# Four 64x64 mixing products in place of two column halves, with three PSUM banks shared by two convolution layers

## The chip, the cores and the metric

The kernel runs on one core of one Trainium2 chip. The metric is the device time of one execution in microseconds (us); shorter is better. The kernel before takes 2804.1 us (median of three runs, 2804.09 to 2806.65).

## What is computed

The input is `x` of shape (16, 64, 128, 128) in float32: 16 images of 64 channels. Four residual layers follow one another, each of the form `x = x + layer(group_norm(x))` with 32 groups of two channels:

```python
# layer 0: channel gram matrix, applied to the image, then a 1x1 convolution
gram = einsum('bcn,bdn->bcd', xf, xf) / N
out  = einsum('oc,bchw->bohw', conv_w, einsum('bcd,bdn->bcn', gram, xf))
# layer 1: Scharr filters in x and y on each channel
out  = abs(conv(x, kx)) + abs(conv(x, ky))
# layer 2: a quarter of the channels shifted left, a quarter right, then 3x3 conv, 64 -> 64, + bias
# layer 3: 3x3 conv 64 -> 64, 1x1 conv 64 -> 64, batch norm over the batch, leaky ReLU, clip to 0..255
```

Layer 3 needs statistics over all 16 images before any output can be written, so the kernel has a last part that reads layer 3's result and its input back from HBM, normalizes, adds and stores.

## The kernel before

**Order of the work.** The order is written out by hand. The program is a list of steps, each with four quarters `q` = 0 to 3, and every engine executes its instructions in program order (`InOrder`). An image goes through four stages that run at the same time on different images: `Gram` (layer 0's statistics), `Front` (layers 0 and 1), `Layer2` and `Layer3`. An image is cut into NS = 8 chunks of R = 8 rows for each image half, and in the middle of the run one step handles one chunk of each of Front, Layer2 and Layer3. Within a quarter the order is Layer3, Layer2, Front, then Gram, then `tick()`, which advances the small chains that turn sums into normalization coefficients. On average a step lasts 17.1 us.

**Layer 0 as one product.** Gram leaves for each image a 64x64 matrix that already contains the residual's identity. `abd` holds it twice on the diagonal of a 128x128 matrix, and the two off-diagonal blocks are zero. Front multiplies the input by it; this is called mixing here. A chunk of input is a tile `x` of 128 partitions (64 channels of the upper image half, 64 of the lower) by 8 rows. `mix(i, g)` takes four of the eight rows (512 columns) with `small_product`: one matmul for each column half of the array, 128 rows by 64 columns each. `po` is one PSUM bank. `mix(i + 2, 0)` stands in quarter 1 and `mix(i + 2, 1)` in quarter 3; ScalarE (ACT) reads `po` with `prepare(i + 2, 0)` in quarter 2 and `prepare(i + 1, 1)` in quarter 0 of the next step, and writes `xh`, on which VectorE (DVE) computes layer 1 (`sobel`).

**Layers 2 and 3.** Each is computed from `one`, a product of odd rows that two output rows share, and `two`, a pair of PSUM banks with what each of the two output rows has for itself. `shared` makes `one` with six matmuls, three on each column half. `own(two[:, n], n, ...)` makes one bank of `two` with five matmuls: two on one column half and three on the other, and the next `own` has it the other way round. The order on the matrix engine (PE) in a step is:

- quarter 0: Layer3 `shared`, Layer3 `own` into `two[:, 0]`
- quarter 1: Layer3 `own` into `two[:, 1]`, Front `mix(i + 2, 0)`
- quarter 2: Layer2 `shared`, Layer2 `own` into `two[:, 1]`
- quarter 3: Layer2 `own` into `two[:, 0]`, Front `mix(i + 2, 1)`

ACT copies `one` with a bias to `c`. DVE empties both banks of `two` with a single instruction that adds `c`: `x<-two,c` in quarter 0 for the chunk of Layer2 that ended in the step before (after two small additions, `two<-two,edges`), and `y<-two,c` in quarter 2 for Layer3. Quarter 0 of DVE also has the first two instructions of `sobel`, quarter 1 has four more, and quarters 2 and 3 have one each.

**PSUM.** There are eight banks: `two` has 2 buffers of two banks, and since the layers take turns each has a pair of its own; `one`, `po`, the gram sums `g` and the small products `bank` have one each.

**Other queues.** SyncE (SP) issues the loads and stores. `load` brings a chunk of `x` with two DMAs, one for each image half. GpSimd (POOL) computes edge terms of layer 2 and issues its `qd` copies.

A float32 matmul shows in the trace as two MATMUL records and two weight loads, since it is done in two passes. The trace gives line 73 (the helper of `InOrder`) for nearly every instruction, so groups are told apart by their tiles.

Of the kernel before, what the change touches and what calls it, by code (L numbers as in the profile page):

```python
# [10 lines left out]
F32 = mybir.dt.float32  # L11
# [5 lines left out]
P = 128  # L17
# [91 lines left out]
def tile_kernel(ctx: ExitStack, tc: tile.TileContext, x, cw_h, w2_t, b2, wbin_t, w1_t, b1, gamma, beta, consts, out):  # L109
# [32 lines left out]
    def flat(ap):  # L142
        return ap.rearrange("p j w -> p (j w)")
# [16 lines left out]
    work = ctx.enter_context(tc.tile_pool(name="work", bufs=2))  # L160
    ring = ctx.enter_context(tc.tile_pool(name="ring", bufs=2))
    stp = ctx.enter_context(tc.tile_pool(name="stp", bufs=2))
    ps_two = ctx.enter_context(tc.tile_pool(name="ps_two", bufs=2, space=PSUM))
    ps_one = ctx.enter_context(tc.tile_pool(name="ps_one", bufs=1, space=PSUM))
    ps_po = ctx.enter_context(tc.tile_pool(name="ps_po", bufs=1, space=PSUM))
    ps_g = ctx.enter_context(tc.tile_pool(name="ps_g", bufs=1, space=PSUM))
# [10 lines left out]
    def small_product(dst, wt, src):  # L177

        for o in (1 - last[0], last[0]):
            pe.matmul(dst[cols(o)], wt[:, cols(o)], src, start=True, stop=True)  # L180
        last[0] = o


    bank = ps_sm.tile([P, 512], F32, name="bank")
# [265 lines left out]
    class Front:  # L450
# [11 lines left out]

        def load(self, i):
            b = self.b
            t = xin.tile([P, R, W], F32, tag="x", name=f"x_{b}_{i}")
            for h in range(2):
                sp.dma_start(flat(t[h * C:(h + 1) * C]), halves(x[b].rearrange("c h w -> (c h w)"), h, i * R, R))
            self.xs[i] = t

        def mix(self, i, g):  # L470
            po = ps_po.tile([P, CP, W], F32, tag="po", name=f"po_{self.b}_{i}_{g}")
            small_product(po, self.abd, self.xs[i][:, g * CP:(g + 1) * CP, :])
            self.po[i, g] = po

        def prepare(self, i, g):
            po = self.po[i, g]
            self.normalized(self.chunk(i)[:, 1 + g * CP:1 + (g + 1) * CP, 1:1 + W], po)
            if g == 0 and i > 0:
                self.normalized(self.chunk(i - 1)[:, R + 1, 1:1 + W], po[:, 0, :])
            if g == 1 and i + 1 < NS:  # L480
                self.normalized(self.chunk(i + 1)[:, 0, 1:1 + W], po[:, CP - 1, :])

        def at(self, i, q):
            b = self.b
            if q == 0:
                if i == -3:

                    self.xe = xin.tile([P, W], F32, tag="xe", name=f"xe_{b}", bufs=1)
                    sp.dma_start(self.xe[lo], x[b][:, HH, :])
                    sp.dma_start(self.xe[hi], x[b][:, HH - 1, :])  # L490
                    sp.dma_start(x2_d[b][0:W].rearrange("(p w) -> p w", p=1), w0[0:1, 0:W])
                if i + 3 < NS:
                    self.load(i + 3)
                if -1 <= i < NS - 1:
                    self.prepare(i + 1, 1)
                if 1 <= i:
                    self.store(i - 1)
                    act.activation(
                        junk.rearrange("p (j w) -> p j w", w=W), self.x2.pop(i - 1), AF.Square,
                        accum_out=self.st[:, 1, i - 1:i],  # L500
                    )
                if i == NS:
                    chains.append(coefficients(self.st, lambda co: coefs2.update({b: co}), b2_sb))
            if q == 1 and -2 <= i < NS - 2:
                if i == -2:
                    self.abd, self.co = lead.pop(b)
                    self.pe = ps_g.tile([P, CP, W], F32, tag="g", name=f"pe_{b}")[:, 0, :]
                    small_product(self.pe, self.abd, self.xe)
                self.mix(i + 2, 0)
            if q == 2:  # L510
                if i == -2:
                    nc.gpsimd.memset(self.chunk(0)[lo, 0, :], 0.0)
                    self.normalized(self.chunk(0)[hi, 0, 1:1 + W], self.pe[hi], hi)
                    self.pel = small.tile([P, W], F32, tag="pel", name=f"pel_{b}", bufs=1)
                    self.normalized(self.pel[lo], self.pe[lo], lo)
                if i == NS - 2:
                    nc.gpsimd.memset(self.chunk(NS - 1)[hi, R + 1, :], 0.0)
                    act.copy(self.chunk(NS - 1)[lo, R + 1, 1:1 + W], self.pel[lo])
            if 0 <= i < NS:
                self.sobel(i, q)  # L520
            if q == 2 and -2 <= i < NS - 2:
                self.prepare(i + 2, 0)
            if q == 3 and -2 <= i < NS - 2:
                self.mix(i + 2, 1)
                self.xs.pop(i + 2)

        def sobel(self, i, q):
            b = self.b
# [96 lines left out]
    class Layer2:  # L625
# [57 lines left out]
        def at(self, i, q):  # L683
# [52 lines left out]
            if q == 2:  # L736
                if 0 <= i < NS:
                    t = self.v[i]
                    one = ps_one.tile([P, CP, W], F32, tag="one", name=f"one2_{b}_{i}")
                    two = ps_two.tile([P, 2, CP, W], F32, tag="two", name=f"two2_{b}_{i}")  # L740
                    self.p[i] = two, one
                    shared(one, self.wi[:, 0], t, m)
                    if closing:
                        small_product(one[:, m, :], w0, t[:, R, :])

                    both = self.wi[:, 1]
                    own(two[:, 1], 1, TO_SLOTS, w2, "d2", m, both)
                    if closing:

                        p = two[:, 1, m:CP]  # L750
                        issue([taps(0, p, [both], [t[:, R:R + 1, :]]), taps(1, p, [both], [t[:, R - 1:R, :]])])
                if 1 <= i < NS:
                    self.square(i - 1)
                if 1 <= i:
                    self.store(i - 1)
# [17 lines left out]
    class Layer3:  # L773
# [37 lines left out]
        def at(self, i, q):  # L811
            b = self.b
            n = b * NS + i
            if q == 0 and 0 <= i < NS:
                self.twin(1)
                t = self.v[i]
                one = ps_one.tile([P, CP, W], F32, tag="one", name=f"one3_{b}_{i}")
                two = ps_two.tile([P, 2, CP, W], F32, tag="two", name=f"two3_{b}_{i}")
                self.p[i] = two, one
                shared(one, w3[:, 2], t)  # L820
                own(two[:, 0], 0, TO_PAIRS, w3, "d3")
            if q == 1:
                if 0 <= i < NS:
                    two, one = self.p[i]
                    own(two[:, 1], 1, TO_PAIRS, w3, "d3")
                    self.v.pop(i)
                    self.c = ring.tile([P, CP * W], F32, tag="c3", name=f"c3_{b}_{i}", bufs=1)
                    act.activation(self.c, flat(one), AF.Identity, bias=b1_sb)
                if i + 1 < NS:
                    self.prepare(i + 1)  # L830
                if 1 <= i:
                    y = self.y.pop(i - 1)
                    for s in range(2):
                        for z in range(2):
                            v = pairs(y_d[b], s)[:, (i - 1) * R:i * R, :].rearrange("c (n z) w -> c z n w", z=2)
                            sp.dma_start(v[:, z], y[s * C:(s + 1) * C, z])
            if q == 2:
                if 0 <= i < NS:
                    y = ring.tile([P, 2, CP, W], F32, tag="y", name=f"y_{b}_{i}")
                    self.y[i] = y  # L840
                    two = self.p.pop(i)[0].rearrange("p s j w -> p s (j w)")
                    dve.scalar_tensor_tensor(
                        y.rearrange("p s j w -> p s (j w)"), two, 1.0,
                        self.c.unsqueeze(1).to_broadcast([P, 2, CP * W]),
                        op0=ALU.mult, op1=ALU.add, accum_out=bn_sum[:, n:n + 1],
                    )
                if i + 1 < NS:
                    difference("d3", 0, self.v[i + 1])
            if q == 3:
                if i + 1 < NS:  # L850
                    self.twin(0)
                    difference("d3", 1, self.v[i + 1])
                if 0 <= i < NS:
                    act.activation(
                        junk, self.y[i].rearrange("p s j w -> p (s j w)"), AF.Square,
                        accum_out=bn_sq[:, n:n + 1],
                    )
# [53 lines left out]
    for step in range(steps):  # L911
        for q in range(4):
# [20 lines left out]
            if step == last_one - NS and q == 0:  # L933
                slices(xw.rearrange("p w c t -> p (w c t)"), 8)
                slices(xh.rearrange("p a j w -> p (a j w)"), 3)
                rest(xin, "x", [R, W], 2)
                rest(xin, "xr", [C // 8, W], 3)
                rest(work, "u", [R + 1, W + 2], 2)
                rest(work, "e", [R, W + 2], 1)
# [93 lines left out]
```

## Time and profile before

| | |
|---|---|
| median of three runs | 2804.1 us |
| the profiled execution: its own time | 2800.37 us |
| the profiled execution: span, first to last instruction | 2798.6 us |
| span in which PE is at 9 tenths or more | about 350 to 2330 us |
| last part, DMA at 400 to 420 GB/s, PE idle | about 2350 to 2800 us |
| mixing (`po<-x,abd`) | 1024 records = 512 matmuls, 386.2 us of PE busy time |
| first and last mixing record | 47.3 us and 2102.7 us |
| Gram products (`pg<-xw`) end | about 1740 us |

"Busy" is the time in which at least one instruction of the engine is under way, and a group's busy time is that of its own records. A matmul record's length includes the passage through the array: records of 512 columns last 590 ns, but two that follow one another on the same part of the array start 427 ns apart. The second distance is what a record costs. Two records on different column halves run side by side. A "wait" is idle time of an engine in front of an instruction, put down to what the profile saw arrive last.

### The profile page before, as it was taken

The page shows a single profiled execution, that of the slowest core. Times are in us where ns is not written, and L with a number is a line of the kernel's source. Part 1 is how long each engine was busy: PE and PEld are TensorE (multiplying, and loading weights), DVE is VectorE, ACT ScalarE, POOL GpSimd, SP SyncE. Part 2 cuts the span into 40 slices and gives each one's busy share as a digit, 9 for nine tenths or more (in the row PEclk, how much of TensorE's full clock was granted, in tenths as well). Part 3 has the DMA queues.
Part 4 walks back from the last instruction along what each step waited for, and adds up shares of the span by engine and source line. Part 5 has one row for each costly group of instructions (what it writes and reads, how often), then busy time and mean ns, then how long its engine had stood idle before and what let it go on. Part 6 is the DMA issues. An engine that isn't in the chain of part 4 may idle for free. (4 is left out here: it accounts for less than half of the span.)

```text
span 2798.6 us, 46299 instructions
## 1 busy us (share of the span) xinstructions
PE 2222.1 (79%) x14772; PEld 1088.8 (39%) x14772; DVE 2201.4 (79%) x3758; ACT 2120.1 (76%) x3171; POOL 859.5 (31%) x1326
## 2 busy tenths in 40 slices
PE   4568899999999999999999999999999995000000
PEld 2323444444444545353534353566666641000000
DVE  3999999898989898989898989999997435333332
ACT  4667779888888888888888888998997667333332
POOL 1035433343434343434343434444444310000000
PEclk7679999999999999999999999999999998555555
DMA  6789878888888888888888777888877767999999
GB/s 168 196 221 233 237 198 237 218 232 212 230 215 221 222 220 219 222 216 227 221 219 227 214 184 197 209 204 214 209 207 187 218 192 273 420 420 420 420 420 387
DMA packets 688880, 685.95 MB, mean 245 GB/s; under 512 B 61744, under 2 KB 590144, under 8 KB 688640
## 3 DMA queue, kind: packets, MB, share of 16 engines
q1 hardware_dynamic: 662656, 614.42, 73.9%
q0 software_dynamic: 24576, 68.12, 10.0%
q8 instruction: 119, 1.95, 0.3%
q14 instruction: 121, 0.99, 0.1%
q10 hardware_dynamic: 1408, 0.46, 0.1%
HBM read 346.23 MB, written 268.44 MB: 220 GB/s over the span
## 5 line engine op out<-in xcount | busy, mean ns | idle before, releaser
L73 PE MATMUL two<-d,w 128*64 128x508 f32 (+2 forms) x2560 | 898.2, 586 | 0.0
L73 PE MATMUL two<-d,wi 128*64 128x508 f32 (+3 forms) x1536 | 626.6, 576 | 0.0
L73 POOL DMA_DIRECT2D qd<-d x512 | 269.8, 529 | 882.2 <-issue 330.0
L73 PE MATMUL two<-qd,pk 128*64 128x512 f32 (+1 forms) x1024 | 518.5, 587 | 1.6 <-DMA qd<-d 1.1
L73 POOL TENSOR_SCALAR edges<-v,co 64x8 f32<-64x8 f32 x512 | 335.2, 655 | 352.5 <-ACT v L73 244.4
L73 PE MATMUL po<-x,abd 128*64 128x512 f32 x1024 | 386.2, 631 | 60.4 <-ACT xh L73 60.4
L73 PEld LDWEIGHTS two<-d,w 128*64 128x64 f32 x2560 | 297.9, 136 | 288.7 <-issue 221.2
L73 PE MATMUL one<-v,w 128*64 128x508 f32 (+2 forms) x1600 | 409.0, 578 | 0.0
L73 PE MATMUL one<-v,wi 128*64 128x508 f32 (+3 forms) x1536 | 407.4, 590 | 0.0
L73 DVE TENSOR_TENSOR d<-v 128x512 f32<-128x512 f32 (+1 forms) x512 | 346.1, 679 | 44.4 <-POOL v L73 17.1
L73 ACT COPY qd<-d 64x512 f32<-64x512 f32 x512 | 315.2, 616 | 21.0 <-DVE d L73 14.5
L73 ACT ACTIVATE xh<-po,co 128x128 f32<-128x128 f32 (+1 forms) x480 | 275.3, 621 | 51.0 <-PE po L73 48.7
L73 DVE SCALAR_TENSOR_TENSOR e<-e 128x1032 f32<-128x1032 f32 (+1 forms) x256 | 313.2, 1223 | 0.0
L73 DVE SCALAR_TENSOR_TENSOR y<-two,c 128x1024 f32<-128x1024 f32 x128 | 156.1, 1219 | 125.6 <-ACT v L73 72.4
L73 PEld LDWEIGHTS two<-d,wi 128*64 128x64 f32 x1536 | 196.1, 135 | 143.2 <-issue 107.7
L73 POOL TENSOR_SCALAR v<-v,kc 128x9 f32<-128x9 f32 x256 | 238.4, 944 | 11.9
L73 ACT ACTIVATE v<-x,co 128x512 f32<-128x512 f32 (+2 forms) x368 | 234.9, 704 | 0.0
L73 PEld LDWEIGHTS one<-v,w 128*64 128x64 f32 x1600 | 163.3, 137 | 177.4 <-issue 130.0
L73 PEld LDWEIGHTS one<-v,wi 128*64 128x64 f32 x1536 | 156.0, 138 | 162.6 <-issue 126.4
L73 ACT ACTIVATE u<-u 128x1024 f32<-128x1024 f32 x128 | 135.4, 1058 | 90.3 <-DVE u L73 89.9
L73 DVE SCALAR_TENSOR_TENSOR u<-xh 128x1170 f32<-128x1170 f32 x128 | 175.7, 1372 | 12.2 <-ACT xh L73 9.8
L73 PEld LDWEIGHTS po<-x,abd 128*64 128x64 f32 x1024 | 111.0, 140 | 175.4 <-ACT xh L73 92.3
(154 smaller groups left out, 3442.4 us busy)
## 6 DMA issues: line engine op xcount, KB each, us to landing
xr<-in_x SPq DMA_DIRECT2D x128, 512.0 KB, 6.7
x<-in_x SPq DMA_DIRECT2D x256, 256.0 KB, 4.0
x_d<-u SPq DMA_DIRECT2D x512, 128.0 KB, 3.6
y_d<-y SPq DMA_DIRECT2D x512, 128.0 KB, 4.0
x_d<-x SPq DMA_DIRECT2D x496, 128.0 KB, 2.5
qd<-d POOLq DMA_DIRECT2D x256, 130.0 KB, 3.0
qd<-d POOLq DMA_DIRECT2D x256, 129.8 KB, 3.6
v<-x_d SPq DMA_DIRECT2D x448, 72.1 KB, 3.0
```

The source lines that it names most:

```text
L73: return self.tc.keep_in_program_order(call(*args, **kwargs))
```

## The change

Mixing is done with four products of 64x64 blocks. The input tile is laid out differently: partitions 0 to 63 hold the first four rows of the chunk and partitions 64 to 127 the last four, each for both image halves (`[P, 2, CP, W]`: image half, row, column). Each of the two load DMAs brings four rows of both halves, with runs of 2 KB where they had 4 KB. `mix(i)` multiplies block (g, g) of `abd` by row group g and image half h, and writes to partitions of column half h in bank g of `po`. The two row groups so write to different banks. All four products stand in quarter 1; the mixing in quarter 3 is gone. The matmul count is the same: four for each chunk.

`po` now has two banks in one buffer. The bank for it is taken from `two`: a fixed tile `three` of three banks replaces both buffers. Layer 2 uses banks 1 and 2 as its pair, Layer 3 banks 0 and 1, so bank 1 belongs to both in turn.

```diff
-    ps_two = ctx.enter_context(tc.tile_pool(name="ps_two", bufs=2, space=PSUM))
+    ps_three = ctx.enter_context(tc.tile_pool(name="ps_three", bufs=1, space=PSUM))
...
+    three = ps_three.tile([P, 3, CP, W], F32, name="three")
...
         def load(self, i):
             b = self.b
-            t = xin.tile([P, R, W], F32, tag="x", name=f"x_{b}_{i}")
-            for h in range(2):
-                sp.dma_start(flat(t[h * C:(h + 1) * C]), halves(x[b].rearrange("c h w -> (c h w)"), h, i * R, R))
+            t = xin.tile([P, 2, CP, W], F32, tag="x", name=f"x_{b}_{i}")
+            v = x[b].rearrange("c (h r) w -> c h (r w)", h=2)
+            for g in range(2):
+                j = (i * R + g * CP) * W
+                sp.dma_start(t[g * C:(g + 1) * C].rearrange("p h r w -> p h (r w)"), v[:, :, j:j + CP * W])
             self.xs[i] = t

-        def mix(self, i, g):
-            po = ps_po.tile([P, CP, W], F32, tag="po", name=f"po_{self.b}_{i}_{g}")
-            small_product(po, self.abd, self.xs[i][:, g * CP:(g + 1) * CP, :])
-            self.po[i, g] = po
+        def mix(self, i):
+            po = ps_po.tile([P, 2, CP, W], F32, tag="po", name=f"po_{self.b}_{i}")
+            x = self.xs.pop(i)
+            order = 1 - last[0], last[0]
+            for g in range(2):
+                for h in order:
+                    pe.matmul(po[cols(h), g], self.abd[cols(g), cols(g)], x[cols(g), h], start=True, stop=True)
+            self.po[i] = po

         def prepare(self, i, g):
-            po = self.po[i, g]
+            po = self.po[i][:, g]
...
-                self.mix(i + 2, 0)
+                self.mix(i + 2)
...
-            if q == 3 and -2 <= i < NS - 2:
-                self.mix(i + 2, 1)
-                self.xs.pop(i + 2)
...
-                    two = ps_two.tile([P, 2, CP, W], F32, tag="two", name=f"two2_{b}_{i}")
+                    two = three[:, 1:3]
...
-                two = ps_two.tile([P, 2, CP, W], F32, tag="two", name=f"two3_{b}_{i}")
+                two = three[:, 0:2]
...
-                rest(xin, "x", [R, W], 2)
+                rest(xin, "x", [2, CP, W], 2)
```

## The prediction, made before the changed kernel was run

> **What bounds the kernel now.** I read the page's busy times first, then a table by stage (the windows view) over one image's period and over the stretch after Gram has ended, then DVE's waits in that period, then the timeline at two places.
>
> ```profile
> PE 2222.1 (79%) x14772; PEld 1088.8 (39%) x14772; DVE 2201.4 (79%) x3758; ACT 2120.1 (76%) x3171; POOL 859.5 (31%) x1326
> ...
> L73 PE MATMUL po<-x,abd 128*64 128x512 f32 x1024 | 386.2, 631 | 60.4 <-ACT xh L73 60.4
> ```
>
> The three engines look equal, and mixing looks like a sixth of PE. Both are averages. The windows say more (span, then PE, PEld, DVE, ACT, POOL busy, clock, DMA share, GB/s):
>
> ```profile
> 1503.50:1640.30 136.80, 135.79 (x926) 61.46 (x924) 127.02 (x226) 122.09 (x191) 50.43 (x82) 1.00 0.81 217
> 1800.00:1960.00 160.00, 160.00 (x802) 102.64 (x800) 155.41 (x236) 145.14 (x229) 76.45 (x109) 1.00 0.81 209
> ```
>
> PE has no idle time, so it sets the pace. But DVE is at 93% and 97%: a faster PE meets it almost at once. Where is DVE's slack? Its waits over that period:
>
> ```profile
> DVE y L73 <- ACT junk L73: 6.8, 2, 3.4
> DVE two L73 <- PE two L73: 2.0, 1, 2.0
> DVE y L73 <- ACT v L73: 0.8, 1, 0.8
> ```
>
> They are all near the end of the image's period, in the two steps that hold Gram's 128 small products. (The `y` waits name ACT, but the timeline has Layer3's last `own` record ending 0.1 us before `y` starts, at 1638.31 + 0.59 against 1639.00; it is PE.) For the rest, from 1503 to 1618, DVE's gaps are all within 0.6 us: **DVE has no slack there**, and PE is ahead of it. How far ahead:
>
> ```profile
> 1595.49 1.88 PE L73 MATMUL two<-d,w 128*64 128x508 f32 x8
> ...
> 1596.18 1.23 DVE L73 SCALAR_TENSOR_TENSOR x<-two,c 128x1024 f32<-128x1024 f32 x1
> ...
> 1597.19 0.59 PE L73 MATMUL two<-qd,pk 128*64 128x512 f32 x1
> ...
> 1597.33 0.08 DVE L73 DVE_READ_ACCUMULATOR x<-two,c 128x1 f32 x1
> ...
> 1599.12 1.03 PE L73 MATMUL po<-x,abd 128*64 128x512 f32 x4
> ```
>
> DVE empties Layer2's pair until 1597.41, while PE is already in Layer3's second `own`: by counting ten records for each `own` it starts at about 1596.3 (on the half that the first `own` uses twice) and streams to 1598.9. With separate pairs that is legal. Over the run I measured this distance, second `own` in full swing minus end of DVE's emptying, in 100 steps: 30 are negative, down to -2.2 us. For Layer2's last `own` against `y` it is negative in a third of 88 steps, down to -2.2 as well.
>
> **What the Trainium skill says.** "TensorEngine Tiling (Array Packing)", Key Properties: tiles of one mode run independently, and changing the mode drains the engine. Its Gotcha 1 adds that different row tiles must write different PSUM banks, which the new `po` does. The trace shows independence for two column halves (records in pairs with one start time), nothing for four blocks. It does show a change of mode, for a 2-row product amid 128x64 ones:
>
> ```profile
> 717.85 0.59 PE L73 MATMUL two<-d,wi 128*64 128x508 f32 x1
> 718.37 0.43 PE L73 MATMUL bank<-rw 2*128 2x64 f32 x2
> 718.73 0.28 PE L73 MATMUL bank<-s,kc 128*64 128x2 f32 x4
> ```
>
> 717.85 to 718.37 is 0.52 where 0.427 is the distance without a change: 0.09 in. Out, the last 64-column record starts at 718.53 by the trace and streams 0.05, and the next starts at 718.73: 0.15, of which 0.03 to 0.05 is a weight load: about 0.12. "PSUM — Partial Sum Buffer", in its section on bank collisions, asks that two engines be kept apart by bank, so bank 1 must be a wait between DVE and PE in both directions. No row of before shows that wait.
>
> **The change part by part.**
>
> *Mixing on PE.* Before: four matmuls in two pairs, each pair 2 x 0.427 = 0.853, so 1.707 a step, half of it in quarter 1 and half in quarter 3. After: four at once, 0.853, plus 0.21 for two mode changes, all in quarter 1. Quarter 1 gets 0.21 longer, quarter 3 0.853 shorter: 0.64 less a step. If PE alone counted, the 102 steps from 400 to 2103 us would give 66 us. Bounds: mode changes from 0 (hidden behind weight loads) to 0.5 (the array's passage of 0.59 - 0.43 = 0.16 each way and a weight load of 0.14); the four from 0.853 to 1.707 (two at a time).
>
> *Bank 1.* Layer3's second `own` must now wait for the end of `x<-two,c`, Layer2's last `own` for that of `y<-two,c`. Behind the waiting matmul on PE stand the mixing, Layer2's `shared`, the Gram pieces and the small products of the chains. Who waits for those? ACT's `prepare` stands behind the absolute values, which need DVE's quarter 1; DVE takes chain products a quarter later. From the end X of `x<-two,c`, DVE has 0.7 + 4 x 1.23 = 5.6 us before `y`, and PE needs 2.6 for its `own`: DVE isn't held up. So in the DVE-bound steps the stall costs nothing by itself; but PE can no longer work ahead, and that lead was being spent in the Gram steps. Also, five matmuls on two halves take 3 x 0.853 = 2.56 once an `own` starts from a standstill, not 2.13.
>
> *One image, from the last stall (X = 1597.41) to DVE's wait at 1639.0*, a stretch that PE decides:
> - second `own` begins at X + 0.1 and takes 2.56, to 1600.06, instead of ending at 1598.91: +1.15
> - two quarter-1 mixings: +0.42
> - two quarter-3 mixings gone: -1.71
>
> Sum -0.14 an image. From 1639.0 to the next X, DVE decides, and nothing of its work changes: 0. Ten images (400 to 1800): **-1 us**. Bounds: no stall (DVE a little earlier), -1.3 an image; a stall of 2.2 as in the worst step, +1 an image.
>
> *1800 to 2110.* PE could go from 15.36 to 14.72 a step; DVE, at 97%, can't. All that it can gain is its own waits there (`d<-v` on POOL, fed through ACT from `one`): 3.9 us by the waits view. I take **-4**; bounds 0 and -9 (all its idle time, 3% of 310).
>
> *Start.* At 52 to 59 us PE and ACT take turns over the one `po` bank, and DVE waits 9.8 us for `xh`. With two banks one turn of about 1 us goes: **-1**; bounds 0 and -2. From 60 to 350 us DVE is busy over 90%: 0.
>
> *2110 to 2350.* Layers 2 and 3 alone, PE-bound, no mixing. From Layer2's end DVE needs 0.4 + 1.3 us; PE takes 4.7 for `shared` and the first `own` before it needs bank 1. No stall: 0. If DVE were 3 us late it would cost.
>
> *Loads.* The same bytes in twice as many runs. They are issued over a step before use and landed in 4.0 us; doubled they'd still be hidden. The `x` buffer comes free in quarter 1 instead of 3, so SP waits less: 0. The last 450 us are DMA-bound and unchanged: 0.
>
> **Sum:** -1 - 4 - 1 = **-6 us** on the profiled execution's 2800.4 (span 2798.6), so 2794.4; the median of the runs, 2804.1, is 3.7 above it, and the forecast on the median is **2798**.
>
> **Rivals.**
> *A. DVE paces, as summed* (0.55): about -6, spread over some 10 to either side because the terms +1.15 and -1.71 nearly cancel.
> *B. The four products run in pairs* (0.17): two column halves at a time as now, and the change doesn't do what it says. Then quarter 1 grows by 1.06 instead of 0.21: per image 1.15 + 2.13 - 1.71 = +1.6, ten images +16, and 20 steps after 1800 at +0.2, +4: **2824, slower**. It decides as soon as a mixing takes over 1.2 us. For it: no trace here has two row groups at work at once, and a float32 matmul is two passes. Against it: on the column halves both passes run beside the other half's. "TensorE: Matmul & The Clock Gate", Part 3, gives packed tiles of rows and columns measured speedups of 3 to 10; not for this type.
> *C. The coupling is free* (0.15): DVE comes a little earlier, no stall precedes the Gram steps: -13 - 4 - 1: **2786**.
> *D. The second wait bites* (0.13): Layer2's last `own`, held by `y` in the image's PE-decided steps, adds its 0.43 of unevenness and about a microsecond of stall, +1.4 an image: -6 + 14, **2812**.
>
> **Numbers.** A difference of 0.2% (5.6 us) is about what a measurement can tell from none. A gives faster 0.30, same 0.23, slower 0.02; B slower 0.16, same 0.01; C faster 0.14, same 0.01; D same 0.02, slower 0.11. In all: faster 0.44, same 0.27, slower 0.29. The range reaches from beyond C (2784) to B (2824). A's own range is 2788 to 2808.
>
> **What the next profile would show.** Four `po` records starting within some 30 ns, and four more 0.43 later: the mixing is right; starts in pairs: B. PE waits in front of `three` naming DVE: the coupling; together tens of us from 400 to 2110 while DVE is over 95% busy: A. No such waits: C. DVE's `y` waits of 3.4 should fall to about 2.5, as the mixing ahead of that `shared` is gone. DVE busy less than now between 400 and 1800 would prove me wrong on who paces, and a gain over 25 us would too.

## The result: 3102 us, 10.6% slower

The changed kernel takes 3102.2 us (median of 4 runs, 3101.6 to 3105.7) against 2804.1 us for the kernel before in the same comparison: ratio 1.1062, 95% interval 1.1046 to 1.1079. The forecast was 2798 us with a range to 2824. The change costs 298 us, and no case of the prediction comes near it.

First the page of the profile after: the busy times, then three groups.

```profile
PE 2267.9 (73%) x14772; PEld 966.5 (31%) x14772; DVE 2207.2 (71%) x3758; ACT 2121.7 (68%) x3171; POOL 1001.2 (32%) x1326
...
L73 PE MATMUL three<-d,w 128*64 128x508 f32 (+2 forms) x2560 | 961.2, 590 | 174.3 <-DVE x L73 174.3
...
L73 DVE TENSOR_TENSOR three<-three,edges 128x8 f32<-128x8 f32 x256 | 44.6, 174 | 402.3 <-PE three L73 397.9
...
L73 PE MATMUL po<-x,abd 64*64 64x512 f32 x1024 | 151.4, 663 | 38.5 <-ACT xh L73 38.5
```

Mixing did what was hoped: 151.4 us of busy time where it had 386.2. But PE fell from 79% busy to 73% and DVE from 79% to 71%: both now wait. The second group is a pair of tiny additions, 44.6 us of work in the whole run, and DVE stands idle for 402.3 us in front of them, put down to PE. In front of `three<-d,w` PE stands idle for 174.3 us, put down to DVE. Each of the two engines waits for the other.

The windows by stage (span, then PE, PEld, DVE, ACT, POOL busy, clock, DMA share, GB/s) show that the waits are everywhere and not in one stage. First the kernel before, then the changed one:

```profile
400.00:1800.00 1400.00, 1387.52 (x9177) 615.40 (x9175) 1305.99 (x2296) 1247.43 (x1950) 527.11 (x844) 1.00 0.83 218
1800.00:2110.00 310.00, 310.00 (x1551) 198.98 (x1549) 301.80 (x450) 283.46 (x448) 144.66 (x206) 1.00 0.80 208
```

```profile
400.00:1800.00 1400.00, 1253.55 (x8131) 534.80 (x8132) 1149.13 (x2022) 1103.75 (x1711) 573.10 (x741) 0.99 0.75 195
1800.00:2110.00 310.00, 275.13 (x1504) 110.84 (x1503) 256.05 (x416) 233.51 (x372) 134.43 (x170) 0.99 0.67 172
```

DVE is at 82% and 83%, where before it was at 93% and 97%. Comparing the end of the same `x` emptying in both traces says where the 302 us of the two profiled executions come from: +5 by 315 us of the kernel before, +211 more up to 1812 (19.2 an image, 2.4 a step), +52 up to 2106 (2.7 a step), and +37 in the last 12 steps, which are of Layers 2 and 3 alone. The last part wins 3 back.

One step in the timeline (start, length, engine, operation; in brackets the idle time in front and what ended it):

```profile
1910.19 2.80 PE L73 MATMUL one<-v,w 128*64 128x512 f32 x12
...
1913.61 1.86 PE L73 MATMUL three<-d,w 128*64 128x508 f32 x6
...
1915.51 0.38 DVE L73 TENSOR_TENSOR three<-three,edges 128x8 f32<-128x8 f32 x2 [2.51 <-PE three L73]
...
1916.01 1.23 DVE L73 SCALAR_TENSOR_TENSOR x<-three,c 128x1024 f32<-128x1024 f32 x1
...
1917.29 0.64 PE L73 MATMUL three<-d,w 128*64 128x512 f32 x1 [1.82 <-DVE x L73]
```

Layer2's last `own`, which makes what the edge additions need, has its last record at 1909.84 and is over at 1910.43. DVE was done with its work before at 1913.00 and could have begun then. It begins at 1915.51, which is 0.04 after the last record of Layer3's **first** `own` (1913.61 + 1.86 = 1915.47). That `own` writes bank 0; the edge additions touch banks 1 and 2. Then PE, with its first `own` done, waits 1.82 us until `x` is emptied, to write bank 1. So in nearly every step (DVE waits so ahead of 119 of the 128 emptyings) `shared`, `own` and the emptying stand one after the other, where they used to run side by side.

**Theory W.** The waits that the program keeps are for the tile `three` as a whole, not for its banks (a bank is an eighth of PSUM, and the unit in which `own` writes). Layer3's first `own` stands ahead of the edge additions in program order, so DVE waits for it, though they share no bank. **Rival S**: the true sharing of bank 1 is what costs, through PE's wait for `x`. **Rival M**: the four-block mixing or its mode changes cost.

### The profile page after: what moved, and what is told of

Read it like the earlier page. It is cut to its first block, busy times and chain, and to the rows that moved or that the text cites. A ratio compares the mean times of both kernels' runs of the same rounds, so it can differ in the third digit from the quotient of the medians.

```text
span 3100.7 us, 46140 instructions
## 1 busy us (share of the span) xinstructions
PE 2267.9 (73%) x14772; PEld 966.5 (31%) x14772; DVE 2207.2 (71%) x3758; ACT 2121.7 (68%) x3171; POOL 1001.2 (32%) x1326
## 5 line engine op out<-in xcount | busy, mean ns | idle before, releaser
L73 PE MATMUL three<-d,w 128*64 128x508 f32 (+2 forms) x2560 | 961.2, 590 | 174.3 <-DVE x L73 174.3
L73 PE MATMUL three<-d,wi 128*64 128x508 f32 (+3 forms) x1536 | 622.3, 587 | 66.2 <-DVE y L73 65.8
L73 PE MATMUL three<-qd,pk 128*64 128x512 f32 (+1 forms) x1024 | 527.8, 597 | 4.1 <-DMA qd<-d 3.3
L73 POOL TENSOR_SCALAR edges<-v,co 64x8 f32<-64x8 f32 x512 | 465.0, 908 | 154.9 <-ACT v L73 84.1
L73 PEld LDWEIGHTS three<-d,w 128*64 128x64 f32 x2560 | 287.8, 136 | 569.7 <-issue 311.5
L73 DVE TENSOR_TENSOR three<-three,edges 128x8 f32<-128x8 f32 x256 | 44.6, 174 | 402.3 <-PE three L73 397.9
L73 PEld LDWEIGHTS three<-d,wi 128*64 128x64 f32 x1536 | 188.1, 137 | 300.7 <-issue 148.8
L73 DVE SCALAR_TENSOR_TENSOR y<-three,c 128x1024 f32<-128x1024 f32 x128 | 155.7, 1216 | 68.3 <-ACT v L73 38.1
L73 ACT ACTIVATE v<-v,co 128x1154 f32<-128x1154 f32 x128 | 171.9, 1343 | 11.2 <-DMA v<-x_d 7.6
L73 PE MATMUL po<-x,abd 64*64 64x512 f32 x1024 | 151.4, 663 | 38.5 <-ACT xh L73 38.5
```

Of the source, the lines that this page charges most:

```text
L73: return self.tc.keep_in_program_order(call(*args, **kwargs))
```

## Experiments

### Sharing without the new mixing, and four banks without sharing

The first kernel takes only the PSUM part of the change and mixes as before. The second does the same with four banks, so that no bank is shared and every layer keeps a pair of its own, in one tile:

```diff
+    three = ps_three.tile([P, 4, CP, W], F32, name="three")   # first kernel: 3 banks
...
-                    two = ps_two.tile([P, 2, CP, W], F32, tag="two", name=f"two2_{b}_{i}")
+                    two = three[:, 2:4]                        # first kernel: 1:3
...
-                two = ps_two.tile([P, 2, CP, W], F32, tag="two", name=f"two3_{b}_{i}")
+                two = three[:, 0:2]
```

> The kernel before with its mixing untouched (one bank for po, two quarters) and only the pairs changed: one three-bank tile, bank 1 in turn for both layers. Theory W (waits are kept for the whole tile `three`, so the emptying x<-three,c waits for Layer3's first own, which writes bank 0 alone, and Layer3's second own waits for that emptying): slow like the changed kernel, and by the old mixing's 0.64 us a step slower still where that chain sets the step: 3150 to 3190 us. Theory S (the sharing of bank 1 as such): also about 3100 to 3190. Theory M (the four-block mixing and its mode changes cost it): 2804, no change.

> The kernel before with its mixing untouched and both pairs kept apart: four banks, none shared, but cut out of one four-bank tile. Theory W: the same waits as in e1_share_only, though no bank is shared: 3150 to 3190 us, and DVE waits in front of three<-three,edges of about 2 to 3 us a step. Theory S: no shared bank, so no change: 2804 us and no such waits.

Measured: 3175.1 us with three banks (ratio 1.1313, 1.1296 to 1.133) and 3169.7 with four (1.1304, 1.1282 to 1.1327). M falls as the main cause, since the loss is there without the new mixing. S falls too: with nothing shared the loss is the same within their intervals, where S had no loss at all. DVE's wait in front of the edge additions, on the page of the four-bank kernel, is even longer than in the changed kernel: 3.7 us for each of the 128 emptyings, where W had said 2 to 3.

```profile
L73 DVE TENSOR_TENSOR three<-three,edges 128x8 f32<-128x8 f32 x256 | 44.6, 174 | 477.5 <-PE three L73 473.1
```

PE's waits in the same kernel (engine, tile, releaser: us in all, times, longest; 400 to 2110 us) can't come from a common bank, since `x` is emptied from banks 2 and 3 and the `own` behind it writes 0 and 1:

```profile
PE three L73 <- DVE x L73: 116.0, 67, 2.1
PE three L73 <- DVE y L73: 73.5, 53, 3.0
```

The new mixing even helps inside this loss: 3175.1 - 3102.2 = 73 us. That is near the 66 us that the prediction gave for the case that PE alone counts; that PE stands on the path in nearly every step here is argued from this, not shown by a run of its own.

### The other order of emission

If W holds, writing Layer2's quarter 0 ahead of Layer3's turns the false wait round without moving an instruction on PE or DVE: in that quarter Layer2 has nothing on PE and Layer3 nothing on DVE.

```diff
-            for stage, at in starts:
+            order = (starts[1], starts[0], starts[2]) if q == 0 else starts
+            for stage, at in order:
```

> The changed kernel with Layer2's quarter 0 emitted ahead of Layer3's. No engine's own order changes; only the direction of the wait does: x<-three,c no longer waits for Layer3's first own, instead that own waits for the emptying. Theory W: the loss goes, 2790 to 2815 us (DVE then paces, as first forecast), and the wait in front of three<-three,edges on PE falls from 298 us to under 60. Theory S: bank 1 is still shared and the second own still behind the emptying: it stays above 3000 us. Theory M: stays at 3102.

> e1_share_only with Layer2's quarter 0 emitted ahead of Layer3's: old mixing, shared bank, wait turned round. Theory W: the coupling alone then costs what a PE that is bound and can't run ahead of DVE loses, 1 to 2 us an image and 0.3 us a step: 2815 to 2850 us; the distance to e3_after_swap is what the four-block mixing is worth (10 to 50 us). Theory S: above 3000 us.

Measured: 2881.6 us for the changed kernel so (1.0268, 1.0253 to 1.0284) and 2848.2 with the old mixing (1.0153, 1.0136 to 1.017). 221 of the 298 us are gone with the order alone, so S is out as the main cause. The second is inside W's range. But W's number for the first was missed by 67 us, and the old mixing is 33 us faster here, where W had the new one ahead. The waits say what was overlooked. From 400 to 2300 us, DVE's and PE's largest in the changed kernel with this order:

```profile
DVE y L73 <- ACT junk L73: 52.6, 18, 3.1
DVE d L73 <- issue: 50.9, 54, 1.5
...
PE three L73 <- DVE x L73: 83.5, 92, 2.5
```

With the order turned, it is Layer3's first `own` (bank 0) that falsely waits for `x` (banks 1 and 2), and everything behind it on PE is late. DVE then waits in front of `d`, which the view puts down to no engine: its next difference overwrites what Layer2's first `own` still reads (tested below, with waits by bank). This cut shows W's direction and is no clean removal.

### Waits by bank

The clean removal declares the pairs on different banks independent and keeps each true wait: the edge additions wait for Layer2's last `own`, Layer3's second `own` for `x`, Layer2's last `own` for `y`. Three kernels: the change itself, the sharing with the old mixing, and four banks with the old mixing. The cut shows the first two; with four banks, where no bank is shared, the remaining pairs are declared too.

```diff
+    def apart(made, group):
+        for a in made:
+            for z in group:
+                tc.declare_no_dep(a.ins, z.ins, reason="other banks")
...
-                        dve.tensor_add(two[:, :, :, w], two[:, :, :, w], e[:, side])
+                        apart([dve.tensor_add(two[:, :, :, w], two[:, :, :, w], e[:, side])], other["own"])
...
+                    apart([xs], other["own"])               # xs: the emptying of x
...
-                    own(two[:, 1], 1, TO_SLOTS, w2, "d2", m, both)
+                    apart(own(two[:, 1], 1, TO_SLOTS, w2, "d2", m, both), other["y"])
...
+                other["own"] = own(two[:, 0], 0, TO_PAIRS, w3, "d3")   # Layer3's first own, bank 0
...
+                    other["y"] = [ys]                       # ys: the emptying of y, banks 0 and 1
```

> The changed kernel in its own order (Layer3 ahead of Layer2 in quarter 0); the pairs of instructions that touch different banks of `three` are declared independent, so only waits between users of one bank are left: DVE's edge additions wait for Layer2's last own, Layer3's second own waits for x's emptying (bank 1), Layer2's last own for y's (bank 1). W (the loss is the waits kept for the whole tile; with waits by bank the sum of the prediction holds): 2790 to 2815 us; DVE waits in front of `three` under 40 us over the run instead of 402, PE waits in front of the second own of a few tenths of a us a step. R (what is left after the change of order, 76 us, is the true coupling over bank 1 with all mixing ahead of Layer2's products): 2850 to 2890 us, with DVE's waits in front of `d` near 50 us from 400 to 2300.

> Layers 2 and 3 share three banks, mixing as before the change (four matmuls in two pairs, in quarters 1 and 3), waits by bank as in the run beside it. W: 2805 to 2830 us, 0 to 25 above that run: with PE waiting for x's end and no mixing time saved, by the prediction's terms +1.15 an image and nothing taken back: 2804 + 12 = 2816. R: 2830 to 2850, and faster than the run beside it by 20 to 40 us, as under the change of order.

> One tile of four banks, two for each layer, none shared, mixing as before the change; the pairs that touch different banks are declared independent. With the waits kept for the whole tile this layout took 3170 us. W: back to the kernel before, 2800 to 2812 us, since nothing but waits differs. If something else in the one tile costs time (its banks' places, its single buffer), clearly above 2812 us.

| waits by bank | median us | ratio to before (95%) |
|---|---|---|
| four banks, old mixing | 2805.3 | 0.9999 (0.9991 to 1.0007) |
| three banks shared, old mixing | 2809.7 | 1.0015 (1.0009 to 1.0022) |
| three banks shared, four-block mixing: the change | 2819.7 | 1.0046 (1.0032 to 1.006) |

The first row is the kernel before again: all that the one tile cost, 3169.7 - 2805.3 = 364 us, was waits between users of different banks. **W is shown.** Of the change's 298 us, 282 go with them, and R falls: the 76 us that were left under the other order are not true coupling. These are the waits from 400 to 2110 us, first in the kernel before, then in the changed kernel with waits by bank. DVE's in front of `three` are as long as those in front of `two` were:

```profile
DVE y L73 <- ACT junk L73: 30.8, 9, 3.4
DVE two L73 <- PE two L73: 17.7, 9, 2.0
...
DVE d L73 <- issue: 3.4, 11, 0.4
```

```profile
DVE y L73 <- ACT junk L73: 22.9, 9, 2.6
DVE d L73 <- issue: 21.6, 18, 1.5
DVE three L73 <- PE three L73: 17.7, 9, 2.0
...
PE three L73 <- DVE x L73: 22.3, 26, 1.8
```

The true sharing of bank 1 costs 5 us, and the four-block mixing on top of it costs 10 more. W's number (up to 2815) is missed by 5, and its order of the last two rows is wrong; R had that order right, with 20 to 40 us between them. Even with the waits that the prediction assumed, the change is 15 us slower by the medians (13 by the ratio), where the sum said 6 us faster. Where do they go?

### Where the last 15 us are

Taking each step's `x` in both traces, the changed kernel with waits by bank keeps pace with the kernel before, to a few hundredths of a us, from step to step, except in the two or three steps of an image with Gram's products, where it loses 1.9 us. From 315 to 1812 us this makes 17.1 us; after 1812 it gains 3.9 in all. (At 315 us it is 7.1 behind, but the profiled execution of the four-bank kernel is 6.2 behind there, and its median is that of the kernel before.) In those Gram steps DVE meets PE at five places, in this order: `y`, `d`, the edge additions, `y`, `d`. DVE's idle time in front of each, in the timelines (0: under 0.15; the last column is a kernel that is explained below):

| DVE waits in front of | before | waits by bank | and a second `d2` buffer |
|---|---|---|---|
| `y` (1618.33 before) | 0.84 | 1.46 | 1.47 |
| `d` | 0.34 | 1.47 | 0 |
| edge additions | 1.97 | 1.97 | 3.53 |
| `y` (1639.00 before) | 3.39 | 2.54 | 2.57 |
| `d` | 0 | 0.93 | 0 |
| sum | 6.54 | 8.37 | 7.57 |

The sums differ by 1.83, which is the loss of an image. Most of it is at `d`, where nothing of the kind was expected: the DVE difference overwrites the half of `d2` that Layer2's first `own` reads. In the kernel before the timeline around this `own` is:

```profile
1615.51 0.59 PE L73 MATMUL two<-d,w 128*64 128x512 f32 x1
...
1617.28 0.59 PE L73 MATMUL po<-x,abd 128*64 128x512 f32 x1
...
1618.13 0.59 PE L73 MATMUL one<-v,wi 128*64 128x512 f32 x1
...
1620.71 0.59 PE L73 MATMUL two<-d,wi 128*64 128x512 f32 x1
```

and in the changed kernel with waits by bank:

```profile
1638.53 0.59 PE L73 MATMUL three<-d,w 128*64 128x512 f32 x1
...
1641.19 1.09 PE L73 MATMUL po<-x,abd 64*64 64x512 f32 x8
...
1642.21 2.79 PE L73 MATMUL one<-v,wi 128*64 128x512 f32 x12
...
1644.83 0.59 PE L73 MATMUL three<-d,wi 128*64 128x512 f32 x1
...
1646.97 0.59 PE L73 MATMUL three<-d,wi 128*64 128x508 f32 x1
...
1647.65 0.69 DVE L73 TENSOR_TENSOR d<-v 128x512 f32<-128x512 f32 x1 [1.47 <-issue]
```

`d` starts 0.09 after the last record of Layer2's first `own` (1646.97 + 0.59 = 1647.56). From Layer3's second `own` to Layer2's first it is 5.20 us before and 6.30 after. An `own` leaves one column half free 0.85 early (two records of 0.427). Before, mixing starts there at once (1617.28, while `own` records still come until 1617.65 + 0.59), and then `shared`. The four blocks need both halves, so they begin only at 1641.19, after all of the `own`. That is 0.85 of the 1.10 more; the mode changes are most of the rest.

To test that `d` is the place, the first of the next kernels gives that half of `d2` a second buffer. The second moves the mixing behind Layer2's first `own`. The third does both, and the fourth gives the buffer to the kernel before.

```diff
-        diffs[name] = wpool.tile([P, 2, CP, W + 2], F32, name=name)
+        diffs[name] = wpool.tile([P, 3 if name == "d2" else 2, CP, W + 2], F32, name=name)
...
-                    apart(own(two[:, 1], 1, TO_SLOTS, w2, "d2", m, both), other["y"])
+                    apart(own(two[:, 1], 1, TO_SLOTS, w2, "d2", m, both, 1 + i % 2), other["y"])
...
-                difference("d2", 1, self.v[i + 1], CP if i + 2 < NS else CP - 1)
+                difference("d2", 1, self.v[i + 1], CP if i + 2 < NS else CP - 1, 1 + (i + 1) % 2)
...
-        junk0 = stp.tile([P, C], F32, tag="junk0", name=f"junk0_{b}", bufs=1)
+        junk0 = stp.tile([P, C], F32, tag="ad", name=f"junk0_{b}", bufs=1)
```

```diff
-                self.mix(i + 2)                  # in quarter 1
...
             if q == 2 and -2 <= i < NS - 2:
+                self.mix(i + 2)
+            if q == 3 and -2 <= i < NS - 2:
                 self.prepare(i + 2, 0)
```

> The changed kernel with waits by bank (2820 us), and a second buffer for the half of `d2` that Layer2's first own reads, so that DVE's next difference needn't wait for that own. P (in the steps with Gram's products PE reaches Layer2's first own 1.1 to 1.7 us later than in the kernel before, because the four blocks need both column halves of the array idle and stand ahead of it, and DVE is then held in front of `d`): DVE's waits in front of `d` put down to issue fall from 21.6 us (400 to 2110) to about 5, an image loses 0.6 to 0.9 us instead of 1.9, the time is 2803 to 2811 us. Q (PE is late anyway; the wait only moves from `d` to `y`): 2815 to 2821 us, with DVE's waits for `y` longer by what those for `d` are shorter.

> The changed kernel with waits by bank; the mixing's four blocks moved from quarter 1 (ahead of Layer2's shared and first own) to quarter 2, behind Layer2's first own, and ACT's first half of prepare from quarter 2 to 3. P: nothing new stands ahead of Layer2's first own, so DVE's waits in front of `d` are near the kernel before's 3.4 us, and the time is 2797 to 2811 us. Q: PE's saved time doesn't show since y waits stay and ACT's prepare is later: 2815 to 2830 us.

> Both edits of the two runs beside it: mixing behind Layer2's first own, and the second buffer for that half of `d2`. P: the two remove the same wait, so within 4 us of the better of the two: 2796 to 2809 us. Q: as the others, 2815 to 2830 us.

> The kernel before with nothing but the second buffer for that half of `d2`. Its DVE waits in front of `d` put down to issue are 3.4 us in all. P and Q: 2800 to 2806 us; if it gains more than 4 us, the buffer does something else than P says, and the run of the changed kernel with it must be read against this one.

| | median us | ratio to before (95%) |
|---|---|---|
| second buffer for `d2` | 2810.6 | 1.0029 (1.0019 to 1.004) |
| mixing behind Layer2's first `own` | 2825.0 | 1.0076 (1.0063 to 1.0088) |
| both | 2828.5 | 1.0088 (1.0074 to 1.0101) |
| the kernel before with the buffer | 2808.1 | 1.0014 (1.0008 to 1.0021) |

*The buffer* takes away the waits for `d` completely and 9 us of the time, as P said. (By the ratios it is 5 us, and their intervals overlap; in the traces the kernel loses 7.5 us from 315 to 1812 us, where it lost 17.1.) In part Q was right too, though not at the place it named. DVE's largest waits, 400 to 2110 us:

```profile
DVE three L73 <- PE three L73: 31.6, 9, 3.5
DVE y L73 <- ACT junk L73: 23.0, 9, 2.6
DVE y L73 <- ACT u L73: 13.3, 9, 1.5
```

In front of the edge additions DVE now waits 31.6 us instead of 17.7: of the 2.4 us that an image no longer waits for `d`, 1.56 come back there (table above). The edge additions need Layer2's last `own`, and the mixing that quarter 3 no longer has stood behind it. The buffer's edit isn't free: it costs the kernel before 4.7 us, 2 us more than forecast. In that trace the kernel is 9.4 us behind at 315 us and 8.3 at 1812, so the cost lies in the start; its cause is open (the edit also lets two small tiles share a buffer). Read against that run, 2810.6 is 2.5 us more (4 by the ratios): with the `d` wait gone, the change still gains nothing.

*Moving the mixing* misses P's number and lands where Q said, for a reason Q gave: ACT's `prepare` comes too late. DVE's largest wait, 400 to 2110 us:

```profile
DVE u L73 <- ACT xh L73: 37.2, 56, 1.1
```

The kernel before has no such wait in that stretch. At `d` P was right: the view shows no wait in front of `d` put down to issue any more, where there were 21.6 us, so the place of the mixing does decide that wait. But mixing can't go behind Layer2's first `own` with `prepare` right after it: what `d` no longer waits, `u` waits and more. No version here beats the kernel before.

## Why the prediction was wrong, point by point

**What bounds the kernel: right for the kernel before, wrong for the one after.** "DVE has no slack there" holds wherever the waits are by bank: there the steps without Gram products run at the same pace. In the changed kernel neither engine paces. The prediction's own test, "DVE busy less than now between 400 and 1800", came out against it: 82% where it was 93%.

**"Mixing on PE": right.** It put 0.853 and 0.21 for the mode changes. Eight `po` records take 1.09 us with the passage (the line at 1641.19), and from the end of the last `own` record's streaming (1641.10) to the next product (1642.21) it is 1.11, against a forecast of 1.06: 0.09 in, 0.93 streaming, 0.09 out. Rival B, blocks in pairs, would have taken 1.7. What the Trainium skill's page "TensorEngine Tiling (Array Packing)" says in Key Properties, that tiles of one mode work independently, holds here for four blocks in float32, and so does the drain at a change of mode. Its price lay in another place than the 0.09: the drain also forbids filling the half that an uneven `own` leaves free, 0.85 us ahead of Layer2's first `own`. In the term "two quarter-1 mixings: +0.42" the second was mis-sized by that: +1.10, not +0.21. (For the first, an `own` from a standstill is already in the +1.15.)

**"Bank 1": the step that failed.** It said that Layer3's second `own` must wait for `x` and Layer2's last `own` for `y`, and stopped there. That is what the banks ask for, and what the Trainium skill's page "PSUM — Partial Sum Buffer" asks for in its section on bank collisions. It isn't all that the program asks for. Replacing two tiles by one made every user of `three` a neighbour of every other. The waits between users of different banks cost 282 us, and the one that decided held DVE for a product of PE in a bank that DVE doesn't touch. "DVE isn't held up" followed from the true waits alone; with those, PE waits 22.3 us for `x` from 400 to 2110 us, the coupling as forecast; none for `y` is listed, so rival D doesn't come true. No row of before could show this, since there each layer's pair was a tile of its own; but the diff showed that two tiles became one, and the order of a quarter (Layer3, then Layer2) showed who would stand in front of whom. Both prices of the new wait should have been worked out, by bank and by tile. The price by tile could be read from the timeline: DVE held until Layer3's first `own` is over, some 5 us after Layer2's last.

**"From the last stall to DVE's wait at 1639.0", -0.14 an image: wrong even with waits by bank.** The +1.15 for the coupling was good. In that trace `x` ends at 1619.81 and the `own` begins at 1619.87; mixing begins 1.27 later than before, both traces laid together at `x`. But the sum was made from end to end, as if PE's late and early parts cancelled. DVE meets PE at several places in between. What DVE loses at one it gets back only where it would have waited for something else later (0.85 of it at the `y` at 1639.00), and the 0.85 that quarter 3 saves comes only after the `d` that needed it. Measured: +1.8 in this stretch and +1.9 in the whole image, instead of -0.14. That the kernel with waits by bank (2819.7) falls inside the stated range is luck: no rival of the prediction names this cost. The prediction's question "Who waits for those?" was answered with ACT's `prepare` and the chains. The missing answer was DVE's difference into `d2`.

**"1800 to 2110", -4: right.** With waits by bank the kernel goes from 24.3 us behind at 1812 to 21.3 behind at 2106 and 20.4 at 2174. It gains at the waits that were named: those in front of `d` put down to POOL are 3.3 us in that stretch before and 1.1 after.

**"2110 to 2350 ... No stall: 0": wrong** for the same false wait, with 37 us in the last 12 steps; with waits by bank nothing is lost there. **"Start", -1,** can't be told: the profiled execution of the four-bank kernel is 6 us behind at 315 us already, though its median is the same as before.

## What to carry to other kernels

Before tiles are merged to save memory, find out whether waits are kept for the tile or for the part of it that is used: a merge can join engines that share nothing, and the cheapest probe is the merge with room enough for all, as with the four banks here. Price a moved piece of work at each place where another engine meets the moved queue, not end to end: a delay ahead of a meeting point isn't paid back by a saving behind it. When DVE or ACT waits, look which record ends just before it starts, and then ask whether the two touch the same memory at all.

## What was not expected of the hardware

Four 64x64 float32 products run wholly side by side, at 1.09 us for all eight records with the passage, where four in pairs of column halves took 1.71 without it. A change of mode costs 0.09 us in each direction, and on top of that whatever one column half would have had to do while the other was still busy: 0.85 us in this kernel.
